# Expert up weights as the stationary operand, fetched for each tile, and small products placed in row and column groups, in a planned 8-sequence float32 network

## The chip, the cores and the metric

The kernel runs on one core of a Trainium2 chip, in one launch. The metric is the device time of that launch in microseconds (us). A core has a matrix engine (PE, whose weight loads are shown apart as PEld), three engines for elementwise work (DVE, ACT and POOL), and an issuing engine for transfers (SP); each works through its own queue of instructions in order and waits on semaphores for the others. SBUF is the core's working memory of 128 partitions; PSUM, in 8 banks of 128 partitions by 512 float32 values, is where PE writes.

## The reference, cut to what matters

All is float32. The input has 8 sequences of 512 tokens of 128 channels. Seven residual steps follow one another; the change touches three kinds of them:

```python
x = x + attn_a0(layernorm(x))      # a linear recurrence
x = x + ffn0(layernorm(x))         # two dense layers with a low-rank term, below
x = x + attn_b0(layernorm(x))      # 4 encoder layers with linear attention
x = x + ffn0(layernorm(x))         # the same low-rank layers again
x = x + attn_a1(layernorm(x))      # causal softmax attention and a dense block
x = x + ffn1(layernorm(x))         # 8 experts, the best 2 of each token
x = x + attn_b1(layernorm(x))      # gated linear attention
x = x + ffn1(layernorm(x))         # the experts again

# ffn0: 8 outer products of token rows are added to each sequence's weights
m1 = (even[:, :4, :, None] * odd[:, :4, None, :]).reshape(B, H, D)
m2 = (even[:, 4:, :, None] * odd[:, 4:, None, :]).reshape(B, D, H)
h = gelu(x @ W1.T + scale * einsum("bsd,bhd->bsh", x, m1) + b1)
out = h @ W2.T + scale * einsum("bsh,boh->bso", h, m2) + b2

# ffn1
scores = rms_norm(x) @ w_router.T            # 8 experts
val, gate = split(rms_norm(x) @ w_up[e].T)   # 2 x 352 of hidden width
y = (val * silu(gate)) @ w_down[e].T         # of the two best experts, weighted by softmax(scores)
```

## The kernel before, in words

The program is not written in the order in which it runs. Python functions describe the steps of each sequence as operations (`f.tensor...`, `f.vector...`, `f.op(...)`) of a planner, the class `Flow`. Each operation has an engine (or two to choose from, `f.either`), a cost in us and a lag until its result can be used. The planner simulates the engines: again and again it takes the operation that can start first, and among equals the one with the lowest rank. A rank is an age, given by `f.turn(name, age)` for each thread of work, plus the PE time that the thread has been given so far. The constants `FIRST` (ages of the 8 sequences in the first part, and an offset for the causal attention) and `LATER` and `AGES` (ages of the parts of the second) set them. PSUM is given out by the planner too, one bank for each `f.ps(...)`. Then all instructions are written out in the planned order, which each engine keeps. `f.several` writes a few matmuls as one operation. Most calls pass through two helper lines, so profile lines show L216 (an operation with one call) and L231 (`several`), and L273 for transfers on SP.

The first part takes the sequences through the recurrence, `lora_steps` (the low-rank layers, 16 times in all), four encoder layers and the causal attention. In `lora_steps` 16 token rows are brought by two small transfers on SP into `tok`, 8 rows each for even and odd; a "spread" makes from the 8 even rows a block-diagonal `even` of 8 x 1024; two products of 512 columns with `tok` as weights give the outer products, and DVE adds them, scaled, to the weights. `tok` and `even` exist once and serve all 16.

The second part works on halves of 4 sequences. In `moe_enter` each sequence's tokens are normalised, saved to DRAM and multiplied by the router's 128 x 8 weights (four products of 8 columns, one for each 128 tokens). `moe_route` chooses two experts a token and gives every choice a slot, sorted by expert; 39 tiles of 128 slots (`TILES`) serve one half. A table of which token fills a slot is made by 32 products of two one-hot matrices (`low`, 128 columns, and `high`, 39). Then `moe_experts` runs, for groups of four tiles: POOL gathers 128 rows for each tile from DRAM (L1983), PE transposes them, and each tile is multiplied by its expert's weights. Which expert that is becomes known at run time: the tile's offset into `experts` (all 8 experts' weights, 8 x 1088 words in each partition, loaded once) is read into a PE register (L2010). The tile is the stationary operand, and two products of 352 columns (L2018, L2019) give gate and value; ACT and DVE form the gated value; three transposes and a copy turn it, and three products (L2028) with the down weights give the result, which POOL scatters back to DRAM (L1993). `moe_combine` loads both results of each token on SP (L2091) and adds them; in the last use it stores the output on SP (L2110). Experts run four times, 156 tiles.

`gated_steps` (four pairs of sequences) has two small products: norms of keys and queries (`pn`, 8 products of 2 columns a pair) and the output's norm (`pz`, 8 products of 1 column a sequence).

SBUF is two large tiles, `left` and `right`, cut by hand for the first part and again for the second.

Of the kernel before, what the change touches and what calls it, by code (L numbers as in the profile page):

```python
# [11 lines left out]
F32 = mybir.dt.float32  # L12
# [8 lines left out]
P = 128  # L21
# [153 lines left out]
class Flow:  # L175
# [93 lines left out]
    def dma(self, out, in_, pick=lambda ap: ap, cost=0.65, lag=2.2, **more):  # L269

        def emit():
            real = lambda v: v.real() if isinstance(v, Ref) else v
            self.nc.sync.dma_start(real(out), pick(real(in_)))  # L273

        return self.op([("sync", cost, emit, None)], [in_], [out], lag=lag, **more)
# [629 lines left out]
def lora_steps(k, f, b, lane, w, pair):  # L905
# [5 lines left out]
    tok, even = pair  # L911
    for e in range(2):
        f.dma(tok[0:8, e, :], n.z[1 + e : 16 + e, 0, :], lambda ap: ap[0:15:2])
    spread = (
        even[0:8],
        tok[0:8, 0:1, :].to_broadcast([8, 8, D]),
        k.ident[0:8, 0:8][:, :, None].to_broadcast([8, 8, D]),
# [5 lines left out]
    p1, p2 = f.ps([P, S]), f.ps([P, S])  # L923
    for h, p in enumerate((p1, p2)):
        f.tensor.matmul(p, tok[:, 1, :], even[:, 4 * h : 4 * h + 4, :].rearrange("p i d -> p (i d)"), start=True, stop=True)
    f.vector.scalar_tensor_tensor(n.w1.rearrange("p c d -> p (c d)"), p1, k.col["scale"], w["w1"], ALU.mult, ALU.add)
    f.vector.scalar_tensor_tensor(
        n.w2, p2.rearrange("p (o c) -> p c o", c=4), k.col["scale"], w["w2"], ALU.mult, ALU.add
    )
    for c in range(4):  # L930
# [818 lines left out]
class MoeLane:  # L1749
# [4 lines left out]
    def __init__(self, base, ints):  # L1754
# [10 lines left out]
        self.off = ints[0:1, 2 * TILES : 3 * TILES]  # L1765
# [8 lines left out]
class ExpertLane:  # L1774


    def __init__(self, base, xn, y, low):
# [4 lines left out]
        self.g, self.gt = [lane.take(3 * P) for i in range(3)], [lane.take(3, P) for i in range(2)]  # L1782
        self.yr = [lane.take(4, D) for i in range(2)]
        self.turn = {}

    WORDS = 1024 + 2048 + 1152 + 768 + 1024

# [5 lines left out]

def scaled(f, out, in_, by):
# [4 lines left out]


def moe_ready(k, f, box):

    for g in box.g:
        f.gpsimd.memset(g, 0.0)


def moe_enter(k, f, w, b, h, box):
# [32 lines left out]
    pr = f.ps([P, NT, E])  # L1840
    for t in range(NT):
        f.tensor.matmul(pr[:, t, :], zt[:, t * P : (t + 1) * P], w["wr"], start=True, stop=True)
# [3 lines left out]
def moe_route(k, f, w, half, h, box):  # L1846
# [69 lines left out]
    v.tensor_scalar(h.ex[0:1], h.ex[0:1], float(E - 1), float(ROW), ALU.min, ALU.mult)  # L1916
    v.tensor_copy(off, h.ex[0:1])
# [22 lines left out]
    pt = f.ps([P, TILES])  # L1940
    for at in range(0, 2 * n, 4):
# [9 lines left out]
            0.9,  # L1951
            [
                ("matmul", (pt, low[:, j, :], h.high[:, at + j, :]), dict(start=(at + j == 0), stop=(at + j == 2 * n - 1)))
                for j in range(4)
            ],
        )
    spare, steps = h.ex, w["iota"][:, 0:TILES]
# [14 lines left out]
def moe_experts(k, f, w, half, h, box):  # L1972
# [34 lines left out]
    def wide(i, held, pg, pv, xt, experts):  # L2007

        def emit():
            o = held[i] = nc.values_load(  # L2010
                off[0:1, i : i + 1].real(),
                engines=[mybir.EngineType.PE],
# [4 lines left out]
            all_of = experts.real()  # L2017
            nc.tensor.matmul(pg.real(), xt.real(), all_of[:, bass.ds(o + HID, HID)], start=True, stop=True)  # L2018
            nc.tensor.matmul(pv.real(), xt.real(), all_of[:, bass.ds(o, HID)], start=True, stop=True)  # L2019
# [3 lines left out]
    def deep(i, held, py, gt, experts):  # L2023

        def emit():
            o, all_of = held[i], experts.real()
            for q in range(3):
                nc.tensor.matmul(  # L2028
                    py.real(),
                    gt[:, q, :].real(),  # L2030
                    all_of[:, bass.ds(o + 2 * HID + q * D, D)],
                    start=(q == 0),
                    stop=(q == 2),
                )

        return emit
# [793 lines left out]
```

## Time and profile before

| | |
|---|---|
| Time, median of 6 runs | 1751.75 us (1749.19 to 1761.98) |
| The profiled execution | 1752.84 us, span 1751.1 us, granted PE clock 0.957 |
| Instructions | 29385 |
| Gathers (L1983) | 156, first at 957.4 us, last at 1706.5 us, 987 ns each on POOL |
| Puts (L1993) | 156, first at 1007.3 us, last at 1731.6 us, 1011 ns each |
| DMA | 54.26 MB, mean 31 GB/s |
| Issues on SP | 32 of the low-rank rows (4 KB, 0.62 us each), 8 of the experts' weights (544 KB), 32 of the combine, 16 of the output |

How to read the profile: an engine's busy time is the union of its instructions. A group's line gives the kernel's line, engine, operation, what it writes and reads, and its shape: 128*32 128x384 is a matmul over 128 rows and 32 columns of the array that moves 384 columns. Behind the bar stand busy time and mean length, then the idle time of the engine just before such instructions and what ended it. A timeline line has start, length, engine, line and how many records were merged. A plain float32 matmul shows as two records.

### The profile page before, as it was taken

Reading aid. Unit: us, or ns where it says so; the run is one execution under the profiler, and the core shown is the slowest. Engines: PE = TensorE matmul, PEld = TensorE weight load, DVE = VectorE, ACT = ScalarE, POOL = GpSimd, SP = SyncE. Lnnn points to the kernel's source line nnn. Section 1 sums busy time; section 2 is a strip of 40 time slices with the busy share of each in tenths; the row PEclk is TensorE's granted clock in tenths of the full one; section 3 lists DMA queues with packets and bytes.
Section 4 is the critical chain, followed back from the end, with each engine's and each line's share of the span. In section 5 each row is a group of like instructions: output and inputs, shape, how many; then the busy total and the mean of one; then the engine's idle time right before and its main releaser. Section 6 shows DMA issues by size and latency. Waiting matters only on the chain.

```text
span 1751.1 us, 29385 instructions
## 1 busy us (share of the span) xinstructions
PE 1593.1 (91%) x10231; PEld 1125.2 (64%) x10231; DVE 1097.4 (63%) x3413; ACT 924.7 (53%) x1824; POOL 836.7 (48%) x976
## 2 busy tenths in 40 slices
PE   4899999999999999999999988889997899977874
PEld 2567776677576666775756556665686666855653
DVE  6687664767566575774766546369775598652523
ACT  1465566655657566466766644257342475422332
POOL 3364353544545344453444565462555534555552
PEclk9899999999999999999999999899998999998997
DMA  5000000000000000010220011120011200111313
GB/s 208 1 1 1 1 7 1 2 1 7 1 7 2 7 1 1 18 41 1 64 64 18 21 39 39 32 85 10 19 44 34 73 24 19 36 35 38 105 36 94
DMA packets 40546, 54.26 MB, mean 31 GB/s; under 512 B 7012, under 2 KB 32101, under 8 KB 40135
## 3 DMA queue, kind: packets, MB, share of 16 engines
q1 hardware_dynamic: 21400, 26.62, 4.8%
q0 software_dynamic: 10256, 21.38, 4.8%
q10 hardware_dynamic: 8736, 4.29, 0.8%
q8 instruction: 86, 1.41, 0.3%
q14 instruction: 68, 0.56, 0.1%
HBM read 33.52 MB, written 18.61 MB: 30 GB/s over the span
## 4 chain that ended last, share of the span: by engine, by line


## 5 line engine op out<-in xcount | busy, mean ns | idle before, releaser
L216 PE MATMUL ps_w<-left 128*128 128x128 f32 (+3 forms) x2540 | 450.3, 321 | 8.4 <-DVE left L216 7.0
L216 PEld LDWEIGHTS ps_w<-left 128*128 128x128 f32 x2540 | 332.1, 193 | 101.6 <-issue 63.8
L216 PE MATMUL ps_w<-right 128*128 128x128 f32 (+2 forms) x1656 | 351.9, 353 | 20.7 <-DVE right L216 13.3
L216 PEld LDWEIGHTS ps_w<-right 128*128 128x128 f32 x1656 | 226.7, 196 | 100.0 <-issue 57.0
L216 ACT ACTIVATE right<-ps_w 128x512 f32<-128x512 f32 (+1 forms) x394 | 207.0, 597 | 94.1 <-PE ps_w L231 74.5
L216 DVE SCALAR_TENSOR_TENSOR left<-left,ps_w 128x352 f32<-128x352 f32 (+1 forms) x220 | 123.1, 565 | 203.1 <-ACT left L216 174.2
L216 ACT COPY left<-ps_w 128x384 f32<-128x384 f32 (+3 forms) x268 | 128.3, 488 | 231.0 <-PE ps_w L216 138.0
L216 ACT ACTIVATE left<-ps_w 128x352 f32<-128x352 f32 (+2 forms) x307 | 157.0, 518 | 159.2 <-PE ps_w L216 63.3
L1993 POOL DMA_INDIRECT rows_out<-left x156 | 157.8, 1011 | 166.2 <-ACT left L216 125.5
L231 PE MATMUL ps_w<-right 128*32 128x512 f32 (+9 forms) x2256 | 201.9, 442 | 9.5 <-DVE right L216 5.5
L2028 PE MATMUL ps_w<-left 128*128 x936 | 142.8, 297 | 60.8 <-issue 30.1
L1983 POOL DMA_INDIRECT left<-rows_in,left x156 | 154.0, 987 | 87.5 <-issue 33.0
L2028 PEld LDWEIGHTS ps_w<-left 128*128 128x128 f32 x936 | 130.7, 206 | 94.1 <-issue 41.4
L216 PE MATMUL ps_w<-w_ident,left 128*128 128x128 f32 x1072 | 180.9, 285 | 8.2 <-DVE left L216 3.5
L216 DVE TENSOR_TENSOR left<-left,ps_w 128x352 f32<-128x352 f32 (+2 forms) x228 | 126.0, 554 | 85.1 <-PE ps_w L216 61.6
L216 PEld LDWEIGHTS ps_w<-w_ident,left 128*128 128x128 f32 x1072 | 133.8, 147 | 61.8 <-issue 25.7
L216 POOL TENSOR_SCALAR_AFFINE_SELECT right<-right 128x512 f32<-128x512 f32 x129 | 82.0, 649 | 165.8 <-ACT right L216 158.0
L231 PEld LDWEIGHTS ps_w<-right 128*32 128x32 f32 (+3 forms) x2256 | 84.8, 149 | 103.3 <-issue 53.6
L2018 PE MATMUL ps_w<-left 128*128 x312 | 133.7, 513 | 9.5 <-ACT left L216 8.3
L2019 PE MATMUL ps_w<-left 128*128 x312 | 126.2, 488 | 0.2 <-ACT left L216 0.2
L216 POOL TENSOR_TENSOR left<-left,mhalf 128x4 f32<-128x4 f32 (+1 forms) x96 | 112.3, 1172 | 18.5 <-DVE left L216 12.4
L216 POOL TENSOR_TENSOR left<-left 128x512 f32<-128x512 f32 x64 | 84.7, 1326 | 40.1 <-ACT left L216 31.8
(114 smaller groups left out, 2196.7 us busy)
## 6 DMA issues: line engine op xcount, KB each, us to landing
left<-rows_out SPq DMA_DIRECT2D x24, 256.0 KB
left<-in_m_dram SPq DMA_DIRECT2D x8, 544.0 KB
rows_in<-left ACTq DMA_DIRECT2D x16, 256.0 KB
left<-in_e_dram SPq DMA_DIRECT2D x4, 850.0 KB
left<-rows_in,left POOLq DMA_INDIRECT x156
rows_out<-left POOLq DMA_INDIRECT x156
x<-in_u_dram SPq DMA_DIRECT2D x8, 256.0 KB
saved<-x SPq DMA_DIRECT2D x8, 256.0 KB
```

What stands on the lines that cost most here:

```text
L216: return lambda: getattr(host, method)(*[real(v) for v in args], **{n: real(v) for n, v in kw.items()})
L231: getattr(host, method)(*[real(v) for v in args], **{n: real(v) for n, v in kw.items()})
L1983: return lambda: nc.gpsimd.indirect_dma_start(out=x.real(), out_offset=None, in_=xs, in_offset=bass.IndirectOffsetOnAxis(ap=h.get[:, i : i ...
L1993: made = nc.gpsimd.indirect_dma_start(out=ys, out_offset=bass.IndirectOffsetOnAxis(ap=h.put[:, i : i + 1].real(), axis=0), in_=y.real(), i ...
L2018: nc.tensor.matmul(pg.real(), xt.real(), all_of[:, bass.ds(o + HID, HID)], start=True, stop=True)
L2019: nc.tensor.matmul(pv.real(), xt.real(), all_of[:, bass.ds(o, HID)], start=True, stop=True)
L2028: nc.tensor.matmul(py.real(), gt[:, q, :].real(), all_of[:, bass.ds(o + 2 * HID + q * D, D)], start=(q == 0), stop=(q == 2),)
```

## The change

It has four parts.

1. **Experts.** Of the experts' weights only the down part stays loaded (`room_m`, 8 x 384 words). For each tile, SP reads the tile's expert offset into a register and fetches the up weights, 128 x 704 words, into one of 8 buffers `up` (`fetch`). They are the stationary operand now, in pieces of up to 128 columns, and the transposed tile moves: six products of 128 columns leave gate and value with the hidden width along the partitions, as the down products need them. So the three transposes and the copy are gone. The PE register is read just ahead of the down products, from a second row of offsets. Gathers and puts are planned with a lag of 4.0 in place of 2.2.
2. **Low-rank products.** The 8 rows are spread over four row groups of 32 partitions, two rows in each (four small transfers in place of two); four products over 32 rows, of 256 columns each, into four PSUM banks, replace two over 128 rows of 512 columns.
3. **Small products.** A helper `narrow` swaps the operands: the small matrix, widened with zeros to 32 columns, is stationary in four column groups, and the tokens move, 128 columns in each; then a copy and a transpose bring the result back to tokens along partitions. The router, `pn` and `pz` use it. The slot table's products are swapped as well, in two column groups of 64; two copies, two transposes and an addition follow.
4. **Ages.** `LATER`, `AGES` and `FIRST` get new values.

```diff
+    tok, even, only = pair
     for e in range(2):
-        f.dma(tok[0:8, e, :], n.z[1 + e : 16 + e, 0, :], lambda ap: ap[0:15:2])
+        for j in range(2):
+            at = 1 + e + 2 * j
+            f.dma(tok[j : j + 97, e, :], n.z[at : at + 13, 0, :], lambda ap: ap[0:13:4], lambda ap: ap[0:97:32])
     spread = (
-        even[0:8],
-        tok[0:8, 0:1, :].to_broadcast([8, 8, D]),
-        k.ident[0:8, 0:8][:, :, None].to_broadcast([8, 8, D]),
+        even,
+        tok[:, 0:1, :].to_broadcast([P, 2, D]),
+        only[:, :, None].to_broadcast([P, 2, D]),
         ALU.mult,
     )
...
-    p1, p2 = f.ps([P, S]), f.ps([P, S])
-    for h, p in enumerate((p1, p2)):
-        f.tensor.matmul(p, tok[:, 1, :], even[:, 4 * h : 4 * h + 4, :].rearrange("p i d -> p (i d)"), start=True, stop=True)
+    ps = [f.ps([P, 2 * D]) for g in range(4)]
+    f.several(
+        "tensor",
+        0.53,
+        [
+            (
+                "matmul",
+                (ps[g], tok[32 * g : 32 * g + 32, 1, :], even[32 * g : 32 * g + 32].rearrange("p i d -> p (i d)")),
+                dict(start=True, stop=True),
+            )
+            for g in range(4)
+        ],
     )
...
+def narrow(k, f, lane, lefts, right, m):
+
+
+    pc = f.ps([P, P])
+    for i, (left, moving) in enumerate(zip(lefts, right)):
+        f.several(
+            "tensor",
+            0.26,
+            [
+                ("matmul", (pc[32 * g : 32 * g + 32], left, moving[:, g * P : (g + 1) * P]), dict(start=(i == 0), stop=(i + 1 == len(lefts))))
+                for g in range(4)
+            ],
+        )
+    flat = lane
+    f_copy(f, flat, pc)
+    pt = f.ps([P, P])
+    f.tensor.transpose(pt, flat, k.ident)
+    return pt.rearrange("p (g c) -> p g c", c=32)[:, :, 0:m]
...
-    pr = f.ps([P, NT, E])
-    for t in range(NT):
-        f.tensor.matmul(pr[:, t, :], zt[:, t * P : (t + 1) * P], w["wr"], start=True, stop=True)
+    pr = narrow(k, f, box.next("thin"), [w["wide"]], [zt], E)
     f.vector.tensor_copy(h.r[:, 0, q * NT : (q + 1) * NT, :], pr)
...
         )
         f.several(
             "tensor",
-            0.9,
+            0.5,
             [
-                ("matmul", (pt, low[:, j, :], h.high[:, at + j, :]), dict(start=(at + j == 0), stop=(at + j == 2 * n - 1)))
+                (
+                    "matmul",
+                    (ph[64 * (j % 2) : 64 * (j % 2) + TILES], h.high[:, at + j, :], low[:, j, :]),
+                    dict(start=(at + j < 2), stop=(at + j >= 2 * n - 2)),
+                )
                 for j in range(4)
             ],
...
+    pts = [f.ps([P, TILES]), f.ps([P, TILES])]
+    for i in range(2):
+        some = slice(64 * i, 64 * i + TILES)
+        f_copy(f, thin[some], ph[some])
+        f.tensor.transpose(pts[i], thin[some], k.ident[some, some])
+    v.tensor_copy(h.src, pts[0])
+    pt = thin[:, 0:TILES]
+    v.tensor_tensor(pt, pts[1], h.src, ALU.add)
     spare, steps = h.ex, w["iota"][:, 0:TILES]
     v.tensor_scalar(h.src, pt, 0.0, None, ALU.is_equal)
...
-    def wide(i, held, pg, pv, xt, experts):
+    def fetch(i, up):
 
         def emit():
-            o = held[i] = nc.values_load(
+            o = nc.values_load(
                 off[0:1, i : i + 1].real(),
-                engines=[mybir.EngineType.PE],
+                engines=[mybir.EngineType.SP],
                 min_val=0,
                 max_val=(E - 1) * ROW,
                 skip_runtime_bounds_check_because="clamped where it is made",
             )
-            all_of = experts.real()
-            nc.tensor.matmul(pg.real(), xt.real(), all_of[:, bass.ds(o + HID, HID)], start=True, stop=True)
-            nc.tensor.matmul(pv.real(), xt.real(), all_of[:, bass.ds(o, HID)], start=True, stop=True)
+            nc.sync.dma_start(up.real(), k.drams["m"][:, bass.ds(o + k.offsets["m"]["experts"][0], 2 * HID)])
 
         return emit
 
-    def deep(i, held, py, gt, experts):
+    def deep(i, py, gt, down):
 
         def emit():
-            o, all_of = held[i], experts.real()
+            o = nc.values_load(
+                off[0:1, TILES + i : TILES + i + 1].real(),
+                engines=[mybir.EngineType.PE],
+                min_val=0,
+                max_val=(E - 1) * 3 * D,
+                skip_runtime_bounds_check_because="clamped where it is made",
+            )
+            all_of = down.real()
             for q in range(3):
+                r = min(P, HID - q * P)
                 nc.tensor.matmul(
-                    py.real(),
-                    gt[:, q, :].real(),
-                    all_of[:, bass.ds(o + 2 * HID + q * D, D)],
-                    start=(q == 0),
-                    stop=(q == 2),
+                    py.real(), gt[0:r, q, :].real(), all_of[0:r, bass.ds(o + q * D, D)], start=(q == 0), stop=(q == 2)
                 )
 
         return emit
 
-    held = {}
-    experts = w["experts"]
...
             h.gathers.append(
-                f.op([("gpsimd", 1.26, get(xr[:, j, :], i), None)], [h.get[:, i : i + 1]], [xr[:, j, :]], after=saved, lag=2.2)
+                f.op([("gpsimd", 1.26, get(xr[:, j, :], i), None)], [h.get[:, i : i + 1]], [xr[:, j, :]], after=saved, lag=4.0)
             )
         pt, py = f.ps([P, 4, P]), f.ps([P, 4, D])
         for j in range(m):
...
-            pg, pv = f.ps([P, HID]), f.ps([P, HID])
-            f.op([("tensor", 1.27, wide(i, held, pg, pv, xt[:, j, :], experts), None)], [xt[:, j, :], off, experts], [pg, pv])
-            f.scalar.activation(g[:, 0:HID], pg, AF.Tanh, scale=0.5)
-            f.vector.scalar_tensor_tensor(g[:, 0:HID], g[:, 0:HID], 1.0, pg, ALU.add, ALU.mult)
-            f.vector.tensor_tensor(g[:, 0:HID], g[:, 0:HID], pv, ALU.mult)
-            pt = f.ps([P, 3, P])
-            for q in range(3):
-                f.tensor.transpose(pt[:, q, :], g[:, q * P : (q + 1) * P], k.ident)
-            f_copy(f, gt, pt)
-            f.op([("tensor", 0.68, deep(i, held, py[:, j, :], gt, experts), None)], [gt, experts], [py[:, j, :]])
+            gt, up = box.next("gt"), box.next("up")
+            f.op([("sync", 1.2, fetch(i, up), None)], [off[:, i : i + 1]], [up], lag=3.4)
+            pg, pv = f.ps([P, 3, P]), f.ps([P, 3, P])
+            for ps, at in ((pg, HID), (pv, 0)):
+                rows = [min(P, 2 * HID - at - q * P) for q in range(3)]
+                f.several(
+                    "tensor",
+                    0.68,
+                    [
+                        ("matmul", (ps[0 : rows[q], q, :], up[:, at + q * P : at + q * P + rows[q]], xt[:, j, :]), dict(start=True, stop=True))
+                        for q in range(3)
+                    ],
+                )
+            f.scalar.activation(gt, pg, AF.Tanh, scale=0.5)
+            f.vector.scalar_tensor_tensor(gt, gt, 1.0, pg, ALU.add, ALU.mult)
+            f.vector.tensor_tensor(gt, gt, pv, ALU.mult)
+            f.op([("tensor", 0.68, deep(i, py[:, j, :], gt, down), None)], [gt, off[:, TILES + i : TILES + i + 1], down], [py[:, j, :]])
         if first + m < TILES:
             scaled(f, yr[:, 0:m, :], py[:, 0:m, :], 0.5)
...
     for i in range(2):
-        for t in range(NT):
-            f.tensor.matmul(pn[:, t, i, :], n.sq[i][:, t * P : (t + 1) * P], w["two"], start=True, stop=True)
-    v.tensor_scalar(n.nn, pn, 1e-24, 4.0, ALU.max, ALU.mult)
+        pn = narrow(k, f, n.thin, [w["two"]], [n.sq[i]], 2)
+        v.tensor_scalar(n.nn[:, :, i, :], pn, 1e-24, 4.0, ALU.max, ALU.mult)
...
-            at = slice(t * P, (t + 1) * P)
-            for vc in range(2):
-                f.tensor.matmul(pz[:, t : t + 1], x2[:, vc, at], w["one"], start=(vc == 0), stop=(vc == 1))
+        pz = narrow(k, f, n.thin, [k.all1[:, 0:32]] * 2, [x2[:, vc, :] for vc in range(2)], 1)
         rs = n.rs[hb]
-        v.tensor_scalar(rs, pz, 0.25 / DI, 1e-5, ALU.mult, ALU.add)
+        v.tensor_scalar(rs[:, :, None], pz, 0.25 / DI, 1e-5, ALU.mult, ALU.add)
         f.gpsimd.tensor_tensor(rs, rs, k.mhalf[:, :NT], ALU.pow)
...
-        room_m = some(8 * 1088)
+        room_m = some(8 * 3 * D)
...
+            of = at + 1088 * i + 704
+            f.dma(room_m[:, 3 * D * i : 3 * D * (i + 1)], k.drams["m"][:, of : of + 3 * D], cost=1.0)
         wg = f.load(k, "g", room_g)
-        box = ExpertLane(room_x, rows, y, low)
+        w["wide"] = room_wide
+        box = ExpertLane(room_x, rows, y, low, other(P))
...
 
...
-
...
-
-FIRST = [30.0, 66.0, 62.0, 89.0, 185.0, 190.0, 210.0, 220.0, 327.0]
...
+
...
+
```

## The prediction

> **What bounds the kernel now.** I read the page's busy shares first, then the same shares by stretch, then what PE waited for, then PE's own instructions in order of time.
>
> ```profile
> PE 1593.1 (91%) x10231; PEld 1125.2 (64%) x10231; DVE 1097.4 (63%) x3413; ACT 924.7 (53%) x1824; POOL 836.7 (48%) x976
> ...
> 100.00:957.00 857.00, 843.27 (x5985) 582.93 (x5988) 561.24 (x1908) 537.59 (x1048) 398.66 (x516) 1.00 0.04 12
> 957.00:1751.00 794.00, 681.19 (x3981) 498.75 (x3973) 466.05 (x1254) 350.83 (x702) 395.60 (x404) 0.92 0.16 43
> ```
>
> The stretch lines give length, then PE, PEld, DVE, ACT and POOL busy, the granted clock, the DMA share and GB/s. There are two kernels here. From 100 to 957 us PE is busy 98% at full clock: whatever leaves PE leaves the time. From 957 us, where the first token gather starts, PE is busy 86% of 794 us at a clock of 0.92; 113 us are idle and some of the rest runs slowly after gaps. There a saving on PE is worth something between nothing and a little more than itself. What PE waits for there:
>
> ```profile
> PE ps_w L2028 <- issue: 30.1, 16, 6.3
> PE ps_w L2028 <- ACT left L216: 29.7, 14, 4.5
> ```
>
> L2028 is the expert's down product. It needs the hidden tile transposed by PE and copied by ACT or DVE; a pipeline of four engines ends in this one wait, 60 us of it in 30 pieces.
>
> Prices on PE come from the distance between starts, since a record's length contains the pipeline's depth. One tile in a calm place:
>
> ```profile
> 1689.12 0.83 PE L2028 MATMUL ps_w<-left 128*128 x6
> 1689.78 0.49 PE L216 MATMUL ps_w<-w_ident,left 128*128 128x128 f32 x3
> 1690.11 0.76 PE L2018 MATMUL ps_w<-left 128*128 x2
> 1690.70 0.76 PE L2019 MATMUL ps_w<-left 128*128 x2
> 1691.30 0.83 PE L2028 MATMUL ps_w<-left 128*128 x6
> ```
>
> A float32 product is two records, a transpose one. Three down products of 128 columns take 0.66 (0.22 each, 0.11 a record), three transposes 0.33, a 352-column product 0.59 and 0.60.
>
> ```profile
> 238.12 1.98 PE L216 MATMUL ps_w<-right 128*128 128x512 f32 x4 [0.80 <-DVE right L216]
> 239.94 0.27 PE L216 MATMUL ps_w<-left 128*128 128x128 f32 x1
> ...
> 1008.85 0.95 PE L216 MATMUL ps_w<-left 128*128 128x8 f32 x8
> 1009.66 0.58 PE L2028 MATMUL ps_w<-left 128*128 x3
> ...
> 453.43 0.66 PE L216 MATMUL ps_w<-w_ident,right 128*128 128x128 f32 x4
> 454.01 0.50 PE L231 MATMUL ps_w<-right 32*128 32x128 f32 x8
> 454.45 0.94 PE L216 MATMUL ps_w<-left 128*128 128x128 f32 x6
> ...
> 965.67 1.02 PE L216 MATMUL ps_w<-right 128*128 128x512 f32 x2
> 966.62 0.43 PE L231 MATMUL ps_w<-right 128*32 128x128 f32 x8
> 966.98 0.82 PE L216 MATMUL ps_w<-right 128*128 128x128 f32 x5
> ```
>
> The first pair is the low-rank product now: 1.82 us. The second is the router: four products of 8 columns take 0.81, as long as four of 128, because the weights are as wide. The other two show groups: four products in row groups (32*128) take 0.44, in column groups (128*32) 0.36, where plain ones would take 0.88. But going in costs: four transposes before a group take 0.58, not 0.44. I put a visit at 0.1 on the way in and, as an estimate from that, 0.1 on the way out.
>
> **Expert up products (156 tiles).** Removed: two 352-column products and three transposes, 0.59 + 0.60 + 0.33 = 1.52 us. Added: six products of at most 128 columns, 12 records at 0.11, 1.34 with rounding up. Gain 0.18 x 156 = 28 us. Down products stay (the third has 96 rows, same records). PE's register load of 0.30 us (156 of them) moves to just ahead of the down products; it runs in the sequencer beside the matmuls before it, as it does now, and I cost it at nothing; uncovered it would be 47 us. Off PE, the copies go: 145 on ACT (68 us) and 11 on DVE (6 us); tanh and two DVE products grow from 352 to 384 elements, 0.03 us each, on engines that are not full.
>
> **The fetches.** Each tile brings 128 x 704 x 4 bytes, 360 KB; 156 of them are 56 MB, while the one load of all experts (8 x 544 KB) shrinks to 1.6 MB. One old 544 KB load sits in this stretch:
>
> ```profile
> 849.50:853.00 3.50, 3.50 (x43) 1.41 (x41) 1.73 (x6) 3.24 (x6) 2.31 (x6) 1.00 0.56 159
> ```
>
> 159 GB/s at a share of 0.56 is 284 GB/s at a full share, so 1.3 us a fetch, 200 us over the 794 us, on top of a share of 0.16: room enough. On SP a fetch is a register load (0.30, priced by PE's) and an issue (0.33 as the old loads'), 0.65 x 156 = 100 us of an idle queue. Eight buffers at 2.2 us a tile put a fetch 17 us ahead, against some 4 us from issue to use, so I cost it at nothing. Behind a waiting fetch on SP stand later fetches and the combine's loads; ahead of it the combine's loads and the output's stores. Gathers and puts on POOL's queue share the DMA engines; a fetch in front of one adds up to 1.3 us, and both are planned with a lag of 4.0 instead of 2.2.
>
> **Low-rank products (16 steps).** 1.82 goes. The trace has row groups of 128 columns at 0.44 and no plain neighbourhood of 256; twice the columns add two passes of 0.107, 0.65. With the visit, 0.85: gain 0.97, 15 us in all, in the stretch that is PE's alone. Bounds: 0.44 (as if 128 columns) to 1.07 (as the 512-column block after 1005.18 us), so 9 to 20 us. Two more SP issues of 0.62 us a step, 20 us on an idle queue; if each waits for the one before, 2 us on a chain that PE's other sequences cover; uncovered, 32 us. The spread falls from 1.3 us on DVE; four evacuations of 256 replace two of 512 at 0.74, about even. Four PSUM banks are held instead of two.
>
> The Trainium skill (TensorE: Matmul & The Clock Gate, on measured speedup of packing) puts four row groups of 32 at 3.07 times, and TensorEngine Tiling (on key properties) warns that a change of mode drains the array. By 3.07 the step would take 0.59 and the part would gain 20 us; by the warning, which has no figure there, less; the rows above carry both, and their 15 us is what I use.
>
> **Small products in column groups.** A narrow product is a block of 0.36, a visit of 0.2 and a transpose of 0.11: 0.67. Router: 0.81 - 0.67 = 0.14, times 16, 2 us. Key norms: 16 records at 0.11 are 1.76, two narrow ones 1.34, times 4, 2 us. Output norms: 1.76 against 0.36 + 0.24 + 0.2 + 0.11 = 0.91, times 8, 7 us. Slot table: eight records are 0.88, a two-pair block in halves 0.42 (by the row form 64*128, whose pairs start 0.42 apart) plus 0.2, gain 0.26 x 32 = 8 us, less two transposes with their visits a route, 2 us. Sum 17. If no visit cost anything, 17 + 0.2 x 72 = 31; if one cost twice this, 3. Each narrow product adds a copy and a transpose, about 1 us, to a chain; that is hidden while experts or other sequences run, and some 5 us are not (the end of each route).
>
> **Stalls and order.** One tile's chain loses three transposes, a copy and two hand-overs, over 1 us. Of the 60 us of waits at L2028 I take 15 as gone (bounds 0 and 60). The ages reorder everything: the first half's second experts (147 to 344) now rank behind the second half's (102 to 146) and become filler. No row prices this. The most a better order can win is PE's idle 113 us; I take nothing and leave 40 either way.
>
> **Sum.** The profiled execution took 1752.84 (span 1751.1 and 1.7 around it; the median shown is 1751.75, 0.1% lower). 1752.8 - 28 - 15 - 17 - 15 + 5 = 1682.8; rounded with the bounds leaning to gains in idle, **1680 us**.
>
> **Rivals.**
> *The second part is not PE's.* In experts-only stretches POOL must issue a gather and a put a tile, 1.01 + 0.99 plus 0.3 each, 2.6 us, more than PE's 2.2. From 1559 to 1751 PE is busy 134.5 of 192. If the 28 us and the 15 of stalls bring nothing, 1752.8 - 15 - 17 + 5 = **1726**. Against it: in that stretch POOL is busy 90 of 192, so it isn't full either.
> *The order gains too.* With the shorter chain and a longer planned lag, a third of the 113 idle us goes beyond my sum: **1640**.
> *Fetches stand behind SP's waits (slower).* SP is in order. Its waits before combine loads (L2091: 57 us) and output stores (L2110: 31 us, longest 16.7) are harmless now, since nothing of PE's is behind them. A fetch is. All of it passed on, with half again for the slower clock after gaps, is 132 us: 1683 + 132 = **1815**; it decides from 70 us of lateness on, that is, with half a microsecond a tile. Against it: the 17 us of lead exceed the longest of these waits. The same sign would come from ages that leave the last experts alone at the end.
> *The change doesn't do what it says*: groups don't overlap here. The blocks above overlap, so I give it nothing.
>
> **Chances.** A measurement of this kernel tells about 0.5% from no change: 1743 to 1760. Forecast (1655 to 1705) 0.48; second part not PE's (1705 to 1743) 0.22; order gains (below 1655) 0.12; between, no change, 0.05; slower 0.13. So faster 0.82. The range 1625 to 1752 leaves out the slower cases and the far end of the gains.
>
> **What would show it.** After: L2018 and L2019's two products replaced by 12 records a tile at 0.11; PE's busy sum down by about 60 us; blocks of 32*128 32x256 near 0.65; ACT's 128x384 copies gone; waits before the down products under 45 us; DMA share in the second part near 0.4; SP's long waits not followed by PE waits on a DMA of `in_m_dram`. Waits on that DMA of over 20 us, or a first part longer than before, would make me wrong.

## The result and the profile after

The changed kernel takes 1773.77 us (median of 20 runs), the kernel before 1751.86 beside it (46 runs): a ratio of 1.0116, interval 1.0097 to 1.0134. It is slower; 1680 was predicted. The profiled execution has a span of 1771.8 us. PE's line of the page and the two stretches that the prediction separated, cut at the first gather (944.9 us, before 957.4):

```profile
PE 1549.7 (87%) x11115; PEld 1147.1 (65%) x11115; DVE 1073.2 (61%) x3427; ACT 896.6 (51%) x1752; POOL 826.2 (47%) x979
...
100.00:945.00 845.00, 820.94 (x5933) 567.62 (x5931) 532.75 (x1903) 553.08 (x1073) 386.47 (x508) 1.00 0.04 13
945.00:1771.00 826.00, 660.93 (x4896) 534.29 (x4892) 469.68 (x1260) 306.14 (x601) 399.82 (x415) 0.90 0.38 106
```

PE's work did go. Its busy time on the page falls by 43 us (1593.1 to 1549.7). Counted from start to start, as the prediction prices it, the fall can only be estimated: 40 to 115 us, by how finely kinds of records are told apart. The first part is 12.5 us shorter, near the 15 of the low-rank products. But the second is 33 us longer, with PE busy 80% of it instead of 86%. What PE waits for there, at the down product (now L2078) and at the gathers:

```profile
PE ps_w L2078 <- DVE left L216: 48.6, 21, 6.1
PE ps_w L2078 <- issue: 11.7, 15, 4.2
PE ps_w L216 <- DMA left<-rows_in,left: 10.0, 4, 9.0
PE ps_w L2078 <- ACT left L216: 4.8, 2, 3.4
```

The wait before the down products, 60.6 us before, is 65.1: the same chain from engine to engine, ended by another engine.

### The profile page after: what moved, and what is told of

Read it like the earlier page. It is cut to its first block, busy times and chain, and to the rows that moved or that the text cites. A ratio compares the mean times of both kernels' runs of the same rounds, so it can differ in the third digit from the quotient of the medians.

```text
span 1771.8 us, 31655 instructions
## 1 busy us (share of the span) xinstructions
PE 1549.7 (87%) x11115; PEld 1147.1 (65%) x11115; DVE 1073.2 (61%) x3427; ACT 896.6 (51%) x1752; POOL 826.2 (47%) x979
## 3 DMA queue, kind: packets, MB, share of 16 engines
q1 hardware_dynamic: 43864, 79.98, 15.2%
## 4 chain that ended last, share of the span: by engine, by line
## 5 line engine op out<-in xcount | busy, mean ns | idle before, releaser
L216 PE MATMUL ps_w<-left 128*128 128x128 f32 (+2 forms) x2412 | 436.5, 326 | 14.0 <-ACT left L216 5.6
L216 ACT ACTIVATE left<-ps_w 128x384 f32<-128x384 f32 (+2 forms) x320 | 167.6, 533 | 381.9 <-PE ps_w L231 167.4
L231 PE MATMUL ps_w<-left 128*128 128x128 f32 (+2 forms) x2000 | 272.2, 297 | 26.8 <-ACT left L216 15.5
L231 PEld LDWEIGHTS ps_w<-left 128*128 128x128 f32 (+2 forms) x2000 | 249.3, 200 | 40.7 <-issue 18.2
L216 DVE SCALAR_TENSOR_TENSOR left<-left,ps_w 128x384 f32<-128x384 f32 (+1 forms) x220 | 127.5, 587 | 188.1 <-ACT left L216 126.9
L231 PE MATMUL ps_w<-right 32*128 32x256 f32 (+8 forms) x2448 | 217.7, 441 | 10.9 <-DVE right L216 6.2
L216 DVE TENSOR_TENSOR left<-left,ps_w 128x384 f32<-128x384 f32 (+2 forms) x224 | 130.1, 584 | 143.2 <-PE ps_w L216 78.9
L2078 PE MATMUL ps_w<-left 128*128 x936 | 148.7, 301 | 65.5 <-DVE left L216 48.6
L2078 PEld LDWEIGHTS ps_w<-left 128*128 128x128 f32 x936 | 127.4, 207 | 85.9 <-DVE left L216 47.8
L231 PEld LDWEIGHTS ps_w<-right 32*128 32x128 f32 (+2 forms) x2448 | 93.3, 152 | 116.1 <-issue 50.1
L216 PE MATMUL ps_w<-w_ident,left 128*128 128x128 f32 x604 | 111.3, 285 | 18.6 <-DMA left<-rows_in,left 10.0
L216 ACT ACTIVATE left<-left 128x127 f32<-128x127 f32 (+1 forms) x196 | 83.3, 482 | 44.0 <-DVE left L216 43.5
```

The lines of the kernel that those rows point to most:

```text
L216: return lambda: getattr(host, method)(*[real(v) for v in args], **{n: real(v) for n, v in kw.items()})
L231: getattr(host, method)(*[real(v) for v in args], **{n: real(v) for n, v in kw.items()})
L2078: nc.tensor.matmul(py.real(), gt[0:r, q, :].real(), all_of[0:r, bass.ds(o + q * D, D)], start=(q == 0), stop=(q == 2))
```

## Experiments

Each call of runs went to one chip, with the kernel before beside them. The calls are of two kinds, and much hangs on this: in five the kernel before took 1643 to 1646 us ("even" below), in three 1739 to 1742, near the 1752 of the result ("late"; what differs in the traces stands below, and why it differs stays open). The record numbers the chips, and the number 4 stands beside the first even call and beside the late call of e13 and e14. Whether that is one chip isn't recorded, so "late" may be a passing condition and not a property of a chip; "even chip" and "late chip" below mean the chip of such a call. Times are compared by ratio within a call (95% intervals); expectations in us that were set against 1752 or 1774 can't be read in an even call.

| run | call | us | before | ratio, interval |
|---|---|---|---|---|
| e1_no_fetch | even | 1632.2 | 1645.7 | 0.9916 [0.9889, 0.9944] |
| e2_old_ages | even | 1670.7 | 1645.7 | 1.0164 [1.0132, 1.0196] |
| e3_groups | even | 1657.5 | 1645.7 | 1.0076 [1.0048, 1.0105] |
| e4_experts | even | 1651.9 | 1645.7 | 1.0042 [1.0024, 1.0061] |
| e5_again | even | 1640.2 | 1643.5 | 0.9970 [0.9945, 0.9995] |
| e6_lean_down | even | 1642.0 | 1643.5 | 0.9981 [0.9954, 1.0008] |
| e7_new_ages | even | 1710.0 | 1643.5 | 1.0394 [1.0332, 1.0457] |
| e8_thin_fetch | even | 1632.0 | 1643.5 | 0.9922 [0.9893, 0.9951] |
| e9_puts_by_sp | even | 1635.4 | 1645.3 | 0.9953 [0.9924, 0.9983] |
| e10_puts_by_sp_lean | even | 1607.5 | 1645.3 | 0.9767 [0.9751, 0.9783] |
| e11_after_puts_by_sp | even | 1618.8 | 1645.3 | 0.9834 [0.9818, 0.9851] |
| e12_thin_and_sp | late | 1662.6 | 1742.3 | 0.9553 [0.9510, 0.9595] |
| e13_thin_fetch_b | late | 1764.0 | 1739.1 | 1.0137 [1.0101, 1.0173] |
| e14_after_puts_b | late | 1672.5 | 1739.1 | 0.9594 [0.9553, 0.9636] |
| e15_pause_third | even | 1704.8 | 1643.2 | 1.0398 [1.0356, 1.0440] |
| e16_touch_each | even | 1634.5 | 1643.2 | 0.9955 [0.9931, 0.9979] |
| e17_touch_b | even | 1634.8 | 1645.1 | 0.9943 [0.9924, 0.9963] |
| e18_before_touch | late | 1750.7 | 1740.0 | 1.0065 [1.0043, 1.0087] |

**Parts of the change.** The ages that are exchanged here:

```diff
-LATER = 700.0
+LATER = 599.0
-AGES = [-33.0, -19.0, -149.0, -22.0, 62.0, 85.0, 147.0, -119.0, 102.0, -157.0]
+AGES = [-81.0, -23.0, -39.0, 10.0, 171.0, -14.0, 344.0, 152.0, -15.0, 146.0]
-FIRST = [30.0, 66.0, 62.0, 89.0, 185.0, 190.0, 210.0, 220.0, 327.0]
+FIRST = [-210.0, 126.0, 122.0, 175.0, 193.0, 190.0, 213.0, 217.0, 282.0]
```

The first run issues only the first 8 fetches, in the changed kernel's order:

```diff
         def emit():
+            if group != "rows1" or i >= 8:
+                return
             o = nc.values_load(
```

> The changed kernel in its own order of instructions, with only the first 8 of the 156 fetches of up weights issued; the later tiles are multiplied by whatever those 8 buffers hold, so the output is not the reference's. 148 register loads and issues on SP and 53 MB of transfers are gone. If the fetches cost the time (late weights, or gathers and puts slowed by the traffic), the kernel comes back by 20 us or more, to 1750 or less. If order and chains cost it, it stays within 8 us of 1774.

> The changed kernel with LATER, AGES and FIRST of the kernel before. If the new ages are at fault, it is faster than 1774 by 15 us or more; if the work itself is at fault (fetches, or the swapped products), it stays within 15 us. PE's busy sum should be that of the changed kernel in both cases, since the work is the same.

> The kernel before with its own ages, with the low-rank products in row groups and the small products in column groups, experts as before. By the sum of my prediction PE loses 32 us: 1720. If what PE sheds goes into idle time in the second part, only the 15 us of the low-rank products remain: 1737. If the planner's new order decides, it can lie 20 us to either side of 1752.

> The kernel before with its own ages, with the stationary up weights fetched for each tile, low-rank and small products as before. By my sum PE loses 28 us and some waits: 1710 to 1725. If fetches or the swapped products are at fault for the changed kernel's time, this one is slower than before by 20 us or more.

> The kernel before with the new LATER, AGES and FIRST alone; it computes everything. If an order is set for one set of costs and is worth little under another, this is slower by 15 us or more (ratio above 1.009). My prediction costed the ages at nothing, plus or minus 40; if that is right in the middle, the ratio is 0.997 to 1.003.

The old ages make the changed kernel 1.9% slower than the new ones do (1.0164 against 0.9970 in another even call); the new ages make the kernel before 3.9% slower. No part alone, in the order that the old ages give it, is faster, where the sum had 32 us of gain for one and 28 for the other. So an order fits one set of costs: its effect, 32 us on the changed kernel and 65 on the one before, is of the size of what the change takes from PE, and with the ages set anew the change as a whole is worth 3 us on an even chip. The rest had to be looked for.

**Is PE what bounds the second part?** One run takes 69 us of PE's work out and nothing else, in the order of before; the next takes 198 us of issue off POOL; the third does both.

```diff
-            for q in range(3):
+            for q in range(1):
                 nc.tensor.matmul(
...
-                    stop=(q == 2),
+                    stop=(q == 0),
...
-            made = nc.gpsimd.indirect_dma_start(
-                out=ys,
-                out_offset=bass.IndirectOffsetOnAxis(ap=h.put[:, i : i + 1].real(), axis=0),
-                in_=y.real(),
-                in_offset=None,
-            )
+            made = nc.sync.dma_start(ys[1 + i * P : 1 + (i + 1) * P, :], y.real())
```

> The kernel before, its order untouched, with the down product left to the first 128 of its 352 hidden rows: four of six records a tile are left out, 4 x 0.11 x 156 = 69 us of PE's work, nothing else changes. If PE bounds the second part, as my sum took it, 55 to 75 us of the time go (ratio 0.955 to 0.967). If the order and the latency of each tile's chain bound it, PE just waits longer: 5 to 30 us go (ratio 0.982 to 0.997), and a PE saving there is worth less than half of itself.

> The kernel before in its own order, each put a plain copy issued by SP to rows 1 + 128 i and following, in place of the scatter issued by POOL; the combine so reads rows of other tokens. Same bytes; POOL loses 156 x (0.97 + 0.30) = 198 us of issue, PE loses nothing. If POOL's issue of gathers and puts (2.5 us a tile) paces the expert stretches, where the run with lean down products had POOL taken for 104 of 107 us, the time falls by 25 to 70 us (ratio 0.957 to 0.985). If the chains of the routes and the order hold the second part, under 10 us go (0.994 to 1.002).

> The same with the down product left to its first 128 of 352 hidden rows, which on its own (POOL still issuing the puts) was worth 1.6 us of 69. If PE and POOL stand behind each other, PE's 69 us count once POOL is out of the way: 20 to 60 us below the run with puts by SP alone. If neither paces the second part, within 8 us of it.

> The changed kernel in its own order with the puts issued by SP in the same way. The change as such was worth 3 us on this kind of chip (0.997). If POOL hid its PE saving, it is worth 20 to 60 us now: a ratio that much below the run of the kernel before with puts by SP. If fetches, visits and the order of the routes ate the saving, the two stand within 8 us of each other.

PE's 69 us alone are worth 1.6 (within the noise, and less than either expectation), POOL's 198 alone 9.9 (just inside the "under 10" that was to speak for chains and order), both together 37.8: each stands behind the other. With the puts off POOL 28 of PE's 69 us come through (1635.4 to 1607.5); what holds the other 41 no run shows. These runs also turn a scatter into a plain copy; that POOL's issue time is what counts is read from its timeline, and no run separates the two. The timeline of POOL in the run with lean down products shows how (start, length, operation, and in brackets the idle time before it):

```profile
1543.68 0.96 POOL L1993 DMA_INDIRECT rows_out<-left  x1 [0.98 <-ACT left L216]
1544.94 0.95 POOL L1993 DMA_INDIRECT rows_out<-left  x1 [0.30 <-issue]
1546.20 0.96 POOL L1993 DMA_INDIRECT rows_out<-left  x1 [0.30 <-issue]
1547.46 0.97 POOL L1983 DMA_INDIRECT left<-rows_in,left  x1 [0.30 <-issue]
1548.74 0.98 POOL L1993 DMA_INDIRECT rows_out<-left  x1 [0.30 <-issue]
```

An indirect issue takes POOL 1.27 us, of which the page calls only 0.97 busy. The last expert run of that kernel, whole:

```profile
1497.00:1604.00 107.00, 93.94 (x447) 66.59 (x446) 55.22 (x124) 54.25 (x114) 79.55 (x82) 0.93 0.29 80
```

82 issues lie in it, POOL's only work there: 79.55 busy and 82 x 0.30 between them are 104 of 107 us. POOL is full while the view gives it 74%. In the changed kernel the same holds on an even chip: 78 issues, 75.30 busy of 105 us, 99 with the pauses. With the puts off POOL the changed kernel stands 1.2% below the kernel before (0.9834 against 0.9953), instead of 0.3%: 16.6 us, between the two expectations (20 to 60, or under 8).

**The fetches.**

```diff
-            nc.sync.dma_start(up.real(), k.drams["m"][:, bass.ds(o + k.offsets["m"]["experts"][0], 2 * HID)])
+            some = 2 * HID if group == "rows1" and i < 8 else 128
+            nc.sync.dma_start(up[:, 0:some].real(), k.drams["m"][:, bass.ds(o + k.offsets["m"]["experts"][0], some)])
```

> The changed kernel itself, run beside the others so that its ratio on this chip is known; it computes everything. Official ratio 1.0116. If fetch traffic is what made it slower (the same kernel with eight fetches was 0.9916 here), the ratio stands again at 1.008 to 1.016 and the difference of some 2% belongs to the fetches. If the chip of the official runs, with its longer PE stalls, made the sign, the ratio here is below 1.0.

> The changed kernel with every fetch issued and waited for as before, but only 128 of its 704 columns moved after the first eight, so the products take what is left in the buffers; a fifth of the bytes, the same issues on SP. If the bytes delay gathers and puts, this stands near the run with eight fetches (0.9916), at 0.990 to 1.000, and gathers land in 2.3 us at the median instead of 2.6 to 3.0. If the issues and waits on SP are what costs, it stands with the changed kernel, 1.008 or more.

With all issues and waits but a fifth of the bytes the kernel is where it is with eight fetches (0.9922 and 0.9916): SP costs nothing that shows, the bytes cost 0.5% (8 us). From a gather's issue to the last of its packets the median is 2.2 us before, 2.3 with thin fetches, 3.0 with whole ones (2.7 in the result). That the 8 us come by way of the gathers isn't shown: PE's waits for them are 13.3 us with thin fetches and 15.2 with whole ones. These and others of PE's waits in the changed kernel on the even chip:

```profile
PE ps_w L216 <- DMA left<-rows_in,left: 15.2, 8, 5.1
PE ps_w L2078 <- DVE left L216: 5.8, 11, 1.2
PE ps_w L216 <- DMA left<-in_m_dram: 2.1, 1, 2.1
```

Here the wait before the down products is nearly gone: 6.6 us, where the sum had taken 15 of 60 off. The program is the same, so the 65.1 us of the result must come from what differs between the two executions.

**One program on two chips.** The result's trace and that of e5_again hold the same instructions in the same order. Up to 1020 us they agree within 1.2 us; from there the result's falls back by 133 us in jerks. One of them, in the result's timeline (some lines left out; "remote" is an event that the profile ties to no instruction):

```profile
1081.89 0.96 POOL L2037 DMA_INDIRECT rows_out<-left  x1 [0.30 <-issue]
...
1082.69 0.39 PE L216 MATMUL ps_w<-left,all 128*128 128x128 f32 x2
...
1083.16 0.96 POOL L2037 DMA_INDIRECT rows_out<-left  x1 [0.30 <-issue]
...
1083.58 0.83 PE L231 MATMUL ps_w<-left 128*128 128x128 f32 x6
...
1084.42 0.97 POOL L2027 DMA_INDIRECT left<-rows_in,left  x1 [0.30 <-issue]
...
1085.70 0.96 POOL L2027 DMA_INDIRECT left<-rows_in,left  x1 [0.30 <-issue]
...
1086.96 0.94 POOL L2027 DMA_INDIRECT left<-rows_in,left  x1 [0.31 <-issue]
1089.71 0.29 DVE L216 COPY left<-ps_w 128x128 f32<-128x128 f32 x1 [4.64 <-remote]
1089.84 0.49 ACT L216 ACTIVATE left<-ps_w 128x384 f32<-128x384 f32 x1 [3.73 <-remote]
...
1090.52 0.80 PE L2078 MATMUL ps_w<-left 128*128 x2 [6.11 <-DVE left L216]
```

and the same instructions on the even chip:

```profile
1072.92 0.39 PE L216 MATMUL ps_w<-left,all 128*128 128x128 f32 x2
...
1073.34 0.29 DVE L216 COPY left<-ps_w 128x128 f32<-128x128 f32 x1
...
1073.81 0.83 PE L231 MATMUL ps_w<-left 128*128 128x128 f32 x6
...
1074.68 0.49 ACT L216 ACTIVATE left<-ps_w 128x384 f32<-128x384 f32 x1 [0.34 <-PE ps_w L231]
```

DVE copies what PE transposed, 0.42 us after it on the even chip, 7.02 us after it in the result, though DVE stood idle for 4.64 us of that. ACT's read of the up product is 6.26 us late instead of 0.87, and PE waits 6.11 us for what comes of them. All this lies in a run of issues on POOL. PE's own records go on at 0.11 us from start to start until 1084.14 us, but their ends are modelled, so the profile doesn't tell whether the product or only its signal was late.

A late result costs PE more than the wait. Here are six records of a down product after a wait, and six without one:

```profile
1710.47 1.65 PE L2078 MATMUL ps_w<-left 128*128 x6 [4.33 <-DVE left L216]
...
1082.91 0.83 PE L2078 MATMUL ps_w<-left 128*128 x6
```

From 945 us on, the same PE work is busy 660.9 us at a granted clock of 0.90 in the result and 614.3 us at 0.95 on the even chip: 47 of the 133 us, the other 86 being idle. So the two kinds of chip also differ in the clock; that it follows from the waits is argued from such rows and from the first part, where it is 1.00 in both, and isn't shown by a run.

I counted every place where DVE, ACT or SP, free and waiting for PE, starts over 1 us later behind PE's record than the same instruction does on an even chip. The result has 44, 174 us in all, within or at the edge of a run of issues 1.27 us apart: 36 of the 44 runs of four or more issues have one, 2 of the 35 shorter ones. The kernel before (against e6_lean_down, the same order) has 32, 104 us. Between two even chips the same count gives at most one place, 1.6 us, though POOL issues in the same runs there. The figures move with the rule that delimits a place (counting only the time in which the late engine stands idle, about 168 us in the result and 64 before); the split between the two kinds of chip doesn't.

The traces also record each semaphore update, and there PE isn't alone. In the second part of the result 825 of PE's 904 updates have a record, and 949 of DVE's 1177; on the even chip 903 of 905 and 1175 of 1178; in the first part all of them on both. So what is disturbed may be signals in general, or their recording, and "late results of PE" names only where it was looked for.

The calls that fell on late chips then took suspects away:

> The changed kernel in its own order with both covers off: puts as plain copies issued by SP, and fetches of 128 of 704 columns after the first eight. The puts off POOL alone gave 0.9834, the bytes off alone were worth 0.5% of the time. If the two are separate charges on the same saving, the sum is 0.978 to 0.980 (1609 to 1613 us where the kernel before takes 1645). If POOL and the fetches were delaying the same gathers, nothing is added to 0.9834. If more than both comes free, below 0.972, PE's whole saving of some 70 us is there and only these two hid it; at 0.978 to 0.98, against 0.9953 for the kernel before with its puts by SP, the change is worth 25 to 28 us of the 70 even so, and the rest is lost in the order and the chains.

> The changed kernel with fetches of 128 of 704 columns after the first eight, once more, for a chip where the kernel before takes some 1745 us and PE's results come late: there the changed kernel was 1.0116 and the one with thin fetches and puts by SP 0.9553, against 0.997 and an expected 0.979 on the chips with 1644 us. If the bytes set off the late results, this falls on such a chip to 0.96 to 0.985; if the bytes only slow gathers, to 1.000 to 1.008. On a chip with 1644 us it is 0.992 again and says nothing new.

> The changed kernel with its puts issued by SP as plain copies, for the same kind of chip. If the scatters (128 rows of 512 bytes by POOL's queue) set off the late results, 0.96 to 0.98 there; if the bytes of the fetches do, 0.99 to 1.00. On a chip with 1644 us it is 0.983 again and says nothing new.

The first run met a late chip (0.9553), so its expectations, set for an even one, can't be read. Thin fetches alone leave all of it (46 places, 165 us, 1.0137): the bytes don't set it off. With the puts off POOL's queue 21 places and 67 us are left, and the kernel is at 0.9594: 5% for what is worth 1.4% on an even chip. The places that are left begin within 3 us of a gather's issue, which says less than it seems, since such stretches are 40% of the time between the first gather and the last. These runs halve the number of POOL's issues as well as taking the scatters away; which of the two counts isn't shown. In that trace the wait before the down products is 39.0 us in place of 65.1, most of it in these two lines:

```profile
PE ps_w L2073 <- DVE left L216: 28.3, 21, 8.7
PE ps_w L2073 <- issue: 8.3, 7, 2.8
```

**Would gaps between issues help?** Four runs put another instruction on POOL ahead of the issues: a power operation ahead of every third in the changed kernel, or a memset ahead of each, in the changed kernel twice and in the kernel before once. The first:

```diff
+    def pause():
+        k.issued += 1
+        if k.issued % 3 == 0:
+            nc.gpsimd.tensor_tensor(k.rest[:, 0:4], k.rest[:, 0:4], k.mhalf[:, 0:4], ALU.pow)
...
+            pause()
             made = nc.gpsimd.indirect_dma_start(
```

> The changed kernel, computing everything, with a small power operation on POOL (128x4, 1.1 us by the other such rows) ahead of every third gather or scatter; 104 of them, 120 us of POOL. In the trace of the changed kernel on the first chip every one of the 43 late results lies in a run of indirect issues on POOL 1.27 us apart; 36 of the 43 runs of four and more have one, 4 of the 39 shorter ones. If the run is what holds PE's results back, cutting the runs takes most of the 174 us of lateness: on a chip where the kernel before takes some 1740 us the ratio falls from 1.012 to 0.97 to 0.995, with the 120 us of POOL partly on the path. If the number of issues counts and not their closeness, it is 1.01 to 1.04 there. On a chip with 1644 us there is nothing to win: 1.000 to 1.03.

> The changed kernel, computing everything, with a memset of 128x8 (0.1 us) on POOL ahead of every gather and scatter, 40 us of POOL in all. If any other instruction between two issues lets PE's results through, 0.95 to 0.98 on a chip with 1740 us; if a real pause is wanted, 1.005 to 1.025 there, as late as the changed kernel. On a chip with 1644 us 0.998 to 1.010.

> The changed kernel with a memset of 128x8 on POOL ahead of every gather and scatter, once more, for a chip where the kernel before takes some 1740 us. If any instruction between two issues lets PE's results through, 0.95 to 0.98 there; if the runs of issues hold them back all the same, 1.005 to 1.025. On a chip with 1644 us it is 0.9955 again.

> The kernel before, computing everything, with the memset of 128x8 on POOL ahead of every gather and scatter and nothing else changed, so that its ratio is the worth of the memsets alone. On a chip where the kernel before takes some 1740 us: 0.94 to 0.98 if any instruction between two issues ends the lateness (110 us of it there), 0.998 to 1.015 if not. On a chip with 1644 us: 0.996 to 1.004, which tells whether the 0.3% by which the two runs with memsets stand below the changed kernel comes from them.

The pause met an even chip alone: POOL's busy time rises by 120 us (831.3 to 950.8) and the time by 65 to 70 (1.0398 against 0.9970), so over half of what is added to POOL comes out at the end. The changed kernel with memsets met even chips both times (0.9955 and 0.9943) and says nothing of lateness. The kernel before with memsets met a late one, and they don't help there (1.0065; 31 places, 87 us, against 32 and 104 without them): some instruction between two issues isn't enough. Whether a longer gap would be stays open, since the pause never met a late chip.

## Why the prediction was wrong, step by step

**PE's side of the sum was about right.** 60 us of PE's work were to go (28, 15 and 17); 43 went by the page's busy time, 40 to 115 by the distance between starts. The low-rank block has the 0.65 us that was worked out, with 0.1 on the way in and 0.1 after it, as this stretch of the result shows (from start to start, four transposes take 0.53 instead of 0.43 and the block's eight records 0.64; the first record behind the block takes 0.21 instead of 0.11):

```profile
124.42 0.60 PE L216 MATMUL ps_w<-w_ident,right 128*128 128x128 f32 x4
124.95 0.71 PE L231 MATMUL ps_w<-right 32*128 32x256 f32 x8
125.59 1.16 PE L216 MATMUL ps_w<-left 128*128 128x128 f32 x8
```

So the visit of 0.2 us, an estimate there, is measured. The DMA share is 0.38 for "near 0.4", and no wait of PE on `in_m_dram` exceeds 2.1 us: SP's waits for buffers that an up product frees, 432.6 us, hold nobody up, and the rival with 1815 has none of the loss.

**The step that failed is "a saving on PE is worth something between nothing and a little more than itself", read as the whole of itself.** On an even chip the second part is paced by POOL and PE in turn, and by something more that no run names: there 69 us of PE are worth 1.6 us as long as POOL issues every gather and put, and 28 us when it issues the gathers alone. That was measured in the order of before, and not on a late chip. The rival "the second part is not PE's" had the place and the price (2.6 us a tile on POOL against 2.2 on PE), and I put it aside because "POOL is busy 90 of 192". That share leaves out 0.30 us behind each issue, and the 192 us were stretched by late results. Its 27 us of gain were still too many: 3 came.

**Fetches at nothing**: SP's side yes, but the bytes cost 8 us. The row had been named (1.3 us in front of a gather) and then not charged; a gather takes 0.7 us longer at the median, though that this is how the 8 us come isn't shown.

**Ages at 0, plus or minus 40**: on the changed kernel the new ages are worth 32 us by these ratios, inside the 40; on the kernel before they cost 65, outside it. The middle can't be told apart from the rest, since each set of costs needs its own order.

**Stalls of 15 us at the down products**: on an even chip 6.6 us of such waits are left in the changed kernel, but the run with lean products, in the old order, has 2.8 there too, and the kernel before with the new ages, all its down products in place, 5.0. So most of the 60 belong to the late chip: what I read as the length of a tile's chain was mostly late results.

**The sign** comes with the chip. Against the even calls the result's chip costs the kernel before 108 us (1751.9 - 1643.5) and the changed one 134 (1773.8 - 1640.2). The difference, 25 us, is more than the 22 by which the change is slower. Why the changed kernel loses more there, with 44 places for 32, isn't settled, nor is how much of the 25 us is lateness and how much the lower clock.

What is left of the predicted 70 us on an even chip: 3 come through, 8 go to the fetched bytes, about 14 to POOL (0.9% between 0.3 and 1.2), and some 45 are left over. This takes the charges to add up, which no even call tested; the last figure is a remainder, and that order and chains take it is a guess.

No version here that computes everything was shown to beat the kernel before on both kinds of chip: the changed kernel, with or without memsets, takes 0.3 to 0.6% less on the even ones, and without them 1.2% more in the result. Plain puts with a gather ahead of the combine, which would take scatters out but leave their number of issues, weren't tried.

## What to carry to other kernels

Before an engine's saving is counted, take work off that engine alone in the old order and time it; if nothing comes, do the same to its neighbour and then to both. Count an engine's issue slots by the distance between starts: an engine shown 74% busy was full. And run the same program in a second call, on another chip if possible, before a loss of 1% is explained by the change.

## What the runs showed of the hardware

In some calls PE's results reach other engines 1 to some 10 us late where POOL issues gathers and scatters one behind the other: 174 us in the result, at most 2 us on the even chips, none in the 900 us without such issues. That POOL's issues bear on it is shown by the run that takes the puts off its queue (67 us left, ratio 1.0116 to 0.9594); whether by their kind or their number, by which path, and what sets the calls apart is open. The runs' times come with a granted clock each, so all were recorded, and no run shows whether the recording has a part in it.

The Trainium skill (DMA: Bandwidth & Descriptors, on SWDGE vs HWDGE vs iDMA) says that descriptors of transfers issued from POOL are computed by software and appended to rings in SBUF, a path which transfers issued from SP or ACT never touch. The runs agree as far as that moving the puts to SP's queue takes away 5% on such a chip; the interference that the page names there is DVE locking POOL out of that state, and no run here shows that.

Fetches of 360 KB on another queue, in place of 66 KB, raise a gather's median from issue to last packet from 2.3 to 3.0 us on an even chip. Entering a row group costs PE 0.1 us and the first work after it 0.1 (the stretch at 124.42 us).
